# Segment attention on one core: loops over chunks of 512 rows beside one straight program for segments under 768 owners

## The chip, the cores and the metric

The kernel runs on one core of one Trainium2 chip. The metric is the device time of one execution in microseconds (us). The kernel before takes 1196.74 us, the median of three runs (1195.85 to 1197.27).

## The reference

Each of 16384 tokens has 256 features and one of 8 segment numbers, which are not sorted. Each segment has 3072 padded slots, and `pos` says which slot a token takes. Two tokens can claim one slot, and then the later one owns it.

```python
q, k, v = feat @ Wq, feat @ Wk, feat @ Wv          # 32, 32 and 256 columns
starts = jnp.searchsorted(bids, jnp.arange(8))
pos = jnp.arange(N) - starts[bids]
qp, kp, vp = pad(q), pad(k), pad(v)                # .at[bids, pos].set
scores = jnp.where(mask[:, None, :], qp @ kp.T, -1e9)
r = (softmax(scores) @ vp)[bids, pos]              # per segment
t = r @ Wt
tn = (t - t.mean(0)) / jnp.sqrt(t.var(0) + 1e-5) * gamma + beta
return feat + relu(tn)
```

## The kernel before

All arithmetic is in 32-bit floats, and a matmul of this type stands in the trace as two rows, called passes below. There are three stages.

**Preparation** (L66 to L323). The index arithmetic runs on VectorE: starts by a binary search, positions, owners of slots, the row that each token reads (`ridx`, L323), and per segment the number of owners `n_bc` and of chunks `nch` (L274). A table `t_rows` in DRAM is filled with zeros by DMAs of 2432 KB each on GpSimd's queue (L117); TR (L63) sets how many. GpSimd's index constants (L122) stand behind the fills in its program, and VectorE waits for them (L123). Wv is multiplied by Wt, so that the attention gives t directly.

**Attention, by segment** (L325 to L481). The number of chunks of 512 rows is loaded into a register of every engine (L338), and two sets of loops run over it. The first loop (L346), once for each chunk, finds the tokens that own the chunk's rows: comparisons with a counter (L351, L352), matmuls `pc` (L371), and short VectorE work (L373 to L381). Four indirect DMAs fetch their features (L385). They are transposed on TensorE (`px`, L397) and multiplied into q and k (`pqk`, L401) and into v times Wt (`pv`, L409). The second pair of loops runs over chunks of queries (L425) and, inside it, over chunks of keys (L430). In each pass of the inner loop, four tiles of 128 queries go through the chain that L434 to L463 write: scores `s` with queries on partitions, their maximum `nm` on VectorE (L438), the exponential `pr` on ScalarE with its sum (L445), four transposes `pT` (L451) and a copy `prT` (L453), so that the keys come onto partitions, four matmuls `po` (L456), and a rescaled sum `acc` (L463). Behind the loop over keys the sum is divided (L467, L470) and stored to `t_rows` (L479).

**Normalisation** (L483 to L541). 128 indirect DMAs on GpSimd fetch every token's row (L510), while matmuls with ones add them up (`ps_m`, L498). Then come the subtraction of the mean (L523), squares (L525) and their sums (`ps_v`, L498), and the output with residual (L538 to L541).

The order inside a loop body is that of a list scheduler, and a loop's body is a scheduling unit of its own: nothing crosses from one pass or one segment to the next.

Of the kernel before, what the change touches and what calls it, by code (L numbers as in the profile page):

```python
# [9 lines left out]
F32 = mybir.dt.float32  # L10
I32 = mybir.dt.int32
# [13 lines left out]
CAP = (LMAX // CH + 1) * CH  # rows kept for a segment: its tokens and at least one zero row  # L25
# [3 lines left out]
def segment_attention_bn_kernel(  # L29
# [23 lines left out]
    J = N // P  # tokens of a partition: token = p * J + j  # L53
# [25 lines left out]
    with ExitStack() as att:  # L79
        keep = att.enter_context(tc.tile_pool(name="keep", bufs=1))  # L80
        # Inclusive counts of a segment's owners along each partition's tokens, then the count in
        # the partitions before, then the partition's first token.
# [10 lines left out]
        with ExitStack() as prep:  # L93
# [7 lines left out]
            PS = LMAX // J  # LMAX tokens are PS partitions  # L101
# [10 lines left out]
            # Rows of the table that no segment fills have values too.  # L112
# [22 lines left out]
            # tri[k, m] = k < m; shift[k, m] = (k == m + PS)  # L135
# [20 lines left out]
            # ---- starts: a binary search by segment, over partitions' first tokens, then over  # L156
            # one partition's tokens ----
# [118 lines left out]
            # A segment's first row: those before it have n + 1 rows each.  # L276
# [49 lines left out]
        seg = att.enter_context(tc.tile_pool(name="seg", bufs=1))  # L326
        work = att.enter_context(tc.tile_pool(name="work", bufs=2))
        qT = seg.tile([DQ, CAP], F32, name="qT")
        kT = seg.tile([DQ + 1, CAP], F32, name="kT")  # and what the mask adds to a key's scores
        vx = seg.tile([P, CAP // P, D], F32, name="vx")  # L330
        qw = seg.tile([DQ + 1, CH], F32, name="qw")  # a chunk of queries, and ones for the mask
        nc.vector.memset(qw[DQ : DQ + 1, :], 1.0)
        acc = seg.tile([P, CT, D], F32, name="acc")
        den = seg.tile([P, CT], F32, name="den")
        nmax = seg.tile([P, CT], F32, name="nmax")  # minus the maximum so far

        for b in range(NB):
            n_chunks = nc.values_load(  # L338
                nch[0:1, b : b + 1],
                min_val=1,  # L340
                max_val=CAP // CH,
                skip_runtime_bounds_check_because="a segment has at most LMAX owners of slots",
            )

            with tc.tile_pool(name=f"psA{b}", bufs=2, space=PSUM) as psA:
                with tc.For_i(0, n_chunks) as c:  # L346
                    ir = iota_r[:, ds(c * CH, CH)]
                    # Which partition holds the token of a row, then which of its tokens.
                    oh = work.tile([P, CH], F32, tag="oh", name=f"oh{b}")
                    ge = work.tile([P, CH], F32, tag="ge", name=f"ge{b}")  # L350
# [4 lines left out]
                    # Rows of no token: an index out of bounds, for which zeros stay.  # L355
                    pad = work.tile([P, CT], F32, tag="pad", name=f"pad{b}")
                    nc.vector.tensor_scalar(
                        pad, rcol[:, ds(c * CT, CT)], n_bc[:, b : b + 1], float(N),
                        ALU.is_ge, ALU.mult,
                    )  # L360
                    nc.vector.tensor_scalar(
                        kT[DQ : DQ + 1, ds(c * CH, CH)],
                        iota_r[DQ : DQ + 1, ds(c * CH, CH)],
                        n_bc[DQ : DQ + 1, b : b + 1], NEG, ALU.is_ge, ALU.mult,
                    )
                    x = work.tile([P, CT, D], F32, tag="x", name=f"x{b}")
                    nc.gpsimd.memset(x, 0.0)  # L367
                    idx = work.tile([P, CT], I32, tag="idx", name=f"idx{b}")
                    for t in range(CT):
                        pc = psA.tile([P, J + 2], F32, tag="pc", name=f"pc{b}")  # L370
                        nc.tensor.matmul(pc, oh[:, ts(t, P)], lcx[:, b, :], start=True, stop=True)  # L371
                        lr = work.tile([P, 1], F32, tag="lr", name=f"lr{b}")
                        nc.vector.tensor_tensor(  # L373
                            lr, rcol[:, ds(c * CT + t, 1)], pc[:, J : J + 1], ALU.subtract
                        )
                        upto = work.tile([P, J], F32, tag="upto", name=f"upto{b}")
                        jc = work.tile([P, 1], F32, tag="jc", name=f"jc{b}")
                        nc.vector.tensor_scalar(
                            upto, pc[:, 0:J], lr, None, ALU.is_le, ALU.add, accum_out=jc
                        )  # L380
                        nc.vector.scalar_tensor_tensor(  # L381
                            idx[:, t : t + 1], pc[:, J + 1 : J + 2], jc, pad[:, t : t + 1],
                            ALU.add, ALU.add,
                        )
                        nc.gpsimd.indirect_dma_start(  # L385
                            out=x[:, t, :],
                            out_offset=None,
                            in_=feat,
                            in_offset=bass.IndirectOffsetOnAxis(ap=idx[:, t : t + 1], axis=0),
                            bounds_check=N - 1,  # L390
                            oob_is_err=False,
                        )
                    xT = work.tile([P, DH, CH], F32, tag="xT", name=f"xT{b}")
                    for h in range(DH):
                        px = psA.tile([P, CH], F32, tag="px", name=f"px{b}")
                        for t in range(CT):
                            nc.tensor.transpose(px[:, ts(t, P)], x[:, t, ts(h, P)], ident)  # L397
                        nc.scalar.copy(xT[:, h, :], px)
                    pqk = psA.tile([2 * DQ, CH], F32, tag="pqk", name=f"pqk{b}")
                    for h in range(DH):  # L400
                        nc.tensor.matmul(  # L401
                            pqk, wqk[:, h, :], xT[:, h, :], start=(h == 0), stop=(h == DH - 1)
                        )
                    nc.vector.tensor_copy(qT[:, ds(c * CH, CH)], pqk[0:DQ, :])
                    nc.vector.tensor_copy(kT[0:DQ, ds(c * CH, CH)], pqk[DQ : 2 * DQ, :])
                    for t in range(CT):
                        pv = psA.tile([P, D], F32, tag="pv", name=f"pv{b}")
                        for h in range(DH):
                            nc.tensor.matmul(  # L409
                                pv, xT[:, h, ts(t, P)], wvt[:, h, :],  # L410
                                start=(h == 0), stop=(h == DH - 1),
                            )
                        nc.scalar.copy(
                            vx[:, ds(c * CT + t, 1), :].rearrange("p x d -> p (x d)"), pv
# [162 lines left out]
```

## Time and profile before

| what | us |
| --- | --- |
| median of three runs | 1196.74 |
| span of the profiled execution, first to last instruction | 1179.1 |
| median less span | 17.6 |
| preparation, to the last index (L323) | 0 to 76.5 |
| attention, to the last division (L470) | 77.5 to 824.6 |
| gathering of rows and mean | 829.1 to 1000.7 |
| variance | 1000.7 to 1063.5 |
| output | 1063.5 to 1179.1 |
| TensorE busy over the span | 699.6 |
| VectorE, ScalarE, GpSimd busy | 454.2, 165.3, 212.9 |

The execution that was profiled has only its span as a time of its own; the runs' times are taken without a profile and contain 17.6 us beside such a span. Rows of groups give busy time, the mean duration of one instruction in ns, and the idle time of the engine ahead of it with what ended it. Rows of the timeline give start, duration, engine, line, and in brackets the idle time ahead of it. PE is TensorE's matmuls, PEld its weight loads, DVE VectorE, ACT ScalarE, POOL GpSimd, SP SyncE. PEclk is the granted clock of TensorE, 1.00 being full.

### The profile page before, as it was taken

Reading aid. Unit: us, or ns where it says so; the run is one execution under the profiler, and the core shown is the slowest. Engines: PE = TensorE matmul, PEld = TensorE weight load, DVE = VectorE, ACT = ScalarE, POOL = GpSimd, SP = SyncE. Lnnn points to the kernel's source line nnn. Section 1 sums busy time; section 2 is a strip of 40 time slices with the busy share of each in tenths; the row PEclk is TensorE's granted clock in tenths of the full one; section 3 lists DMA queues with packets and bytes.
Section 4 is the critical chain, followed back from the end, with each engine's and each line's share of the span. In section 5 each row is a group of like instructions: output and inputs, shape, how many; then the busy total and the mean of one; then the engine's idle time right before and its main releaser. Section 6 shows DMA issues by size and latency. Waiting matters only on the chain. (4 is left out here: it accounts for less than half of the span.)

```text
span 1179.1 us, 9985 instructions
## 1 busy us (share of the span) xinstructions
PE 699.6 (59%) x1835; PEld 365.8 (31%) x1835; DVE 454.2 (39%) x1028; ACT 165.3 (14%) x375; POOL 212.9 (18%) x220
## 2 busy tenths in 40 slices
PE   2028465867568684686657765747577776990000
PEld 1015233444334452254434434424111111340000
DVE  4863233334324332333332334223000000918998
ACT  0002010212112220121102211202000000540000
POOL 4010103000110001100030000110677775000000
PEclk9998676787767786687866877668555565895555
DMA  9910100000100001000000000010333332003896
GB/s 348 333 66 1 37 19 19 1 18 0 35 8 1 18 0 37 7 0 19 18 25 1 1 18 18 15 35 1 103 99 101 103 99 84 1 0 142 303 329 258
DMA packets 25441, 80.12 MB, mean 68 GB/s; under 512 B 4674, under 2 KB 11819, under 8 KB 21301
## 3 DMA queue, kind: packets, MB, share of 16 engines
q0 software_dynamic: 12816, 38.85, 10.4%
q1 hardware_dynamic: 8901, 23.19, 6.0%
q10 hardware_dynamic: 3680, 17.63, 3.7%
q14 instruction: 33, 0.27, 0.1%
q8 instruction: 11, 0.18, 0.1%
HBM read 40.82 MB, written 40.50 MB: 69 GB/s over the span
## 5 line engine op out<-in xcount | busy, mean ns | idle before, releaser
L456 PE MATMUL po<-vx,prT 128*128 x640 | 188.4, 452 | 14.6 <-ACT prT L453 14.6
L456 PEld LDWEIGHTS po<-vx,prT 128*128 128x128 f32 x640 | 138.4, 225 | 85.6 <-issue 33.1
L434 PE MATMUL s<-kT,qw 33*128 x160 | 120.9, 869 | 68.3 <-DVE den L428 53.5
L498 PE MATMUL ps_m<-tt,ones 128*128 128x512 f32 x128 | 125.4, 1083 | 52.4 <-DMA tt<-t_rows,ridx 52.2
L510 POOL DMA_INDIRECT tt<-t_rows,ridx x128 | 127.6, 997 | 65.9 <-issue 65.9
L463 DVE SCALAR_TENSOR_TENSOR acc<-acc,fade,po 128x256 f32<-128x256 f32 x80 | 38.4, 480 | 132.7 <-PE po L456 132.7
L371 PE MATMUL pc<-lcx,oh 128*128 128x130 f32 x96 | 29.9, 465 | 98.7 <-DVE oh L352 92.0
L438 DVE TENSOR_REDUCE nm<-s 128x1 f32<-128x512 f32 x80 | 55.3, 691 | 82.6 <-PE s L434 82.5
L498 PEld LDWEIGHTS ps_m<-tt,ones 128*128 128x128 f32 x128 | 30.9, 299 | 145.7 <-issue 103.5
L367 POOL MEMSET x<- 128x1024 f32 x12 | 11.4, 951 | 351.0 <-PEq L338 223.9
L492 DVE COPY mean<-ps_m 128x256 f32<-128x256 f32 x1 | 0.4, 424 | 174.8 <-PE ps_m L498 174.8
L451 PE MATMUL pT<-ident,pr 128*128 128x128 f32 x320 | 59.6, 332 | 13.1 <-ACT pr L445 13.1
L434 PEld LDWEIGHTS s<-kT,qw 33*128 33x128 f32 x160 | 33.3, 243 | 100.6 <-DVE den L428 58.3
L451 PEld LDWEIGHTS pT<-ident,pr 128*128 128x128 f32 x320 | 49.0, 176 | 45.3 <-ACT pr L445 38.5
L429 POOL MEMSET acc<- 128x1024 f32 x12 | 11.4, 951 | 281.1 <-POOLq L425 193.0
L498 PE MATMUL ps_v<-sq,ones 128*128 128x512 f32 x128 | 58.2, 619 | 5.6 <-ACT sq L525 5.6
L385 POOL DMA_INDIRECT x<-in_r_feat,idx x48 | 48.1, 1001 | 72.1 <-DVE idx L381 61.4
L397 PE MATMUL px<-ident,x 128*128 128x128 f32 x96 | 32.5, 444 | 46.1 <-DMA x<-in_r_feat,idx 46.0
L525 ACT ACTIVATE sq<-tt 128x2048 f32<-128x2048 f32 x16 | 30.6, 1910 | 204.8 <-DVE tt L523 184.1
L441 ACT ACTIVATE fade<-nmax,nm 128x1 f32<-128x1 f32 x80 | 23.5, 294 | 240.2 <-DVE nm L439 240.1
L371 PEld LDWEIGHTS pc<-lcx,oh 128*128 128x128 f32 x96 | 22.8, 312 | 106.9 <-DVE oh L352 86.4
L445 ACT ACTIVATE pr<-s,nm 128x512 f32<-128x512 f32 x80 | 53.4, 668 | 0.0
(166 smaller groups left out, 671.2 us busy)
## 6 DMA issues: line engine op xcount, KB each, us to landing
t_rows<-zero POOLq DMA_DIRECT2D x7, 2432.0 KB, 37.5
f<-in_r_feat SPq DMA_DIRECT2D x16, 1024.0 KB, 7.4
out<-y ACTq DMA_DIRECT2D x16, 1024.0 KB, 7.6
t_rows<-tq SPq DMA_DIRECT2D x12, 512.0 KB, 3.0
tt<-t_rows,ridx POOLq DMA_INDIRECT x128, 2.8
x<-in_r_feat,idx POOLq DMA_INDIRECT x48, 2.8
wv_sb<-in_L_rec_Wv ACTq DMA_DIRECT2D x1, 256.0 KB, 13.5
wt_sb<-in_L_rec_Wt ACTq DMA_DIRECT2D x1, 256.0 KB, 18.8
```

The source lines that it names most:

```text
L371: nc.tensor.matmul(pc, oh[:, ts(t, P)], lcx[:, b, :], start=True, stop=True)
L385: nc.gpsimd.indirect_dma_start(out=x[:, t, :], out_offset=None, in_=feat, in_offset=bass.IndirectOffsetOnAxis(ap=idx[:, t : t + 1], axis=0 ...
L397: nc.tensor.transpose(px[:, ts(t, P)], x[:, t, ts(h, P)], ident)
L434: nc.tensor.matmul(s, qw[:, ts(t, P)], kT[:, ds(kc * CH, CH)], start=True, stop=True)
L438: nc.vector.tensor_reduce(nm, s, AX.X, ALU.max, negate=True)
L445: nc.scalar.activation(pr, s, AF.Exp, bias=nm, accum_out=rsum)
L451: nc.tensor.transpose(pT[:, ts(u, P)], pr[:, ts(u, P)], ident)
L456: nc.tensor.matmul(po, prT[:, ts(u, P)], vx[:, ds(kc * CT + u, 1), :].rearrange("p x d -> p (x d)"), start=(u == 0), stop=(u == CT - 1),)
L463: nc.vector.scalar_tensor_tensor(acc[:, t, :], acc[:, t, :], fade, po, ALU.mult, ALU.add)
L498: nc.tensor.matmul(ps, ones, x[:, 2 * h : 2 * h + 2, :], start=(g == 0 and h == 0), stop=(g == J // GT - 1 and h == GT // 2 - 1),)
L510: nc.gpsimd.indirect_dma_start(out=tt[g][:, i, :], out_offset=None, in_=t_rows, in_offset=bass.IndirectOffsetOnAxis(ap=ridx[:, j : j + 1], ...
L525: nc.scalar.activation(sq, tt[g], AF.Square)
```

## The change

The attention stage is written a second time, for segments of fewer than FW = 768 owners, as one program without loops. The largest number of owners is reduced from `n_bc` and loaded into a register of every engine; if it is under 768, the new program runs. It gathers the reciprocals of all denominators in `rdens`, and behind the last segment counts those that are not between 1e-30 and 1e30 into `bad`. `bad` is 1 ahead of the test, so that it also stands for the case of a longer segment. Then `bad` is loaded on every engine, and the code of before runs only if it is over 0. The table grows by 256 rows before rounding, which makes eight fills of it in place of seven.

In the new program each segment has 768 rows (FT = 6 tiles of 128) whatever its owners, and two chunks of 384 queries (QC). Scores are computed with keys on partitions, so `pr` needs no transposes. The exponential takes no maximum, and what masks the keys beyond the owners is its bias per partition. Queries beyond the owners are set to zero. A column of ones in `v` gives the denominator as column 257 of `po`. All six key tiles add up in one PSUM tile, so `acc`, `fade` and `den` go. Segments are interleaved: `project(b + 1)` and `load_rows(b + 2)` stand ahead of `attend(b)`.

```diff
-    TR = -(-(N + NB + CH) // (P * FB)) * P * FB
+    TR = -(-(N + NB + FW) // (P * FB)) * P * FB
...
+        bad = keep.tile([P, 1], I32, name="bad")
+        nc.vector.memset(bad, 1)
+        nc.vector.tensor_reduce(longest, n_bc[0:1, :], AX.X, ALU.max)
+        nc.vector.tensor_copy(longest_i, longest)
+        n_max = nc.values_load(longest_i[0:1, 0:1], ...)
+        with tc.If(n_max < FW):
+                ps_a = short.enter_context(tc.tile_pool(name="ps_a", bufs=1, space=PSUM))
+                ps_s = short.enter_context(tc.tile_pool(name="ps_s", bufs=3, space=PSUM))
+                ps_o = short.enter_context(tc.tile_pool(name="ps_o", bufs=2, space=PSUM))
+                xs = [fs.tile([P, FT, D], F32, name=f"xs{i}") for i in range(2)]
+                vs = [fs.tile([P, FT, D + 1], F32, name=f"vs{i}") for i in range(2)]
...
+                def load_rows(b):
+                    nc.vector.tensor_scalar(ge, ir, lcx[:, b, J : J + 1], None, ALU.is_ge)
+                    nc.vector.scalar_tensor_tensor(oh, ir, cend[:, b : b + 1], ge, ALU.is_lt, ALU.mult)
...
+                    for h in range(FT // 3):
+                        pc = ps_a.tile([P, 3, J + 2], F32, tag="pc", name=f"pc_{b}")
+                        for t in range(3):
+                            nc.tensor.matmul(pc[:, t, :], oh[:, ts(3 * h + t, P)], lcx[:, b, :], ...)
...
+                    for t in range(FT):
+                        nc.gpsimd.indirect_dma_start(out=x[:, t, :], in_=feat, ...)
+                def project(b):
+                    for c in range(FT // 2):
+                        for h in range(DH):
+                            px = ps_a.tile([P, 2 * P], F32, tag="px", name=f"px_{b}", bufs=2)
+                            for t in range(2):
+                                nc.tensor.transpose(px[:, ts(t, P)], x[:, 2 * c + t, ts(h, P)], ident)
+                            if h == 0:
+                                nc.scalar.copy(xT[:, h, ts(c, 2 * P)], px)
+                            else:
+                                nc.vector.tensor_copy(xT[:, h, ts(c, 2 * P)], px)
+                    for c in range(FW // QC):
+                        pqk = ps_a.tile([2 * DQ, QC], F32, tag="px", name=f"pqk_{b}", bufs=2)
...
+                        nc.vector.scalar_tensor_tensor(q[:, own], iota_r[0:DQ, own], n_bc[0:DQ, b : b + 1], pqk[0:DQ, :], ALU.is_lt, ALU.mult)
+                        nc.scalar.copy(k[:, own], pqk[DQ : 2 * DQ, :])
+                    for c in range(FT // 2):
+                        pv = ps_a.tile([P, 2, D], F32, tag="px", name=f"pv_{b}", bufs=2)
...
+                        nc.scalar.copy(v[:, 2 * c : 2 * c + 2, 0:D], pv)
+                def attend(b):
+                    for c in range(FW // QC):
+                        for t in range(FT):
+                            s = ps_s.tile([P, QC], F32, tag="s", name=f"s_{b}")
+                            nc.tensor.matmul(s, k[:, ts(t, P)], q[:, ts(c, QC)], start=True, stop=True)
+                            nc.scalar.activation(pr[:, t, :], s, AF.Exp, bias=mask[:, t : t + 1])
+                        for u in range(QC // P):
+                            po = ps_o.tile([P, D + 1], F32, tag="po", name=f"po_{b}")
+                            for t in range(FT):
+                                nc.tensor.matmul(po, pr[:, t, ts(u, P)], v[:, t, :], ...)
+                            nc.vector.reciprocal(rden, po[:, D : D + 1])
+                            nc.vector.tensor_scalar(tq[:, u, :], po[:, 0:D], rden, None, ALU.mult)
...
+                        nc.sync.dma_start(t_rows[ds(first_row, QC), :].rearrange("(t p) d -> p t d", p=P), tq)
+                load_rows(0)
+                project(0)
+                load_rows(1)
+                for b in range(NB):
+                    if b + 1 < NB:
+                        project(b + 1)
+                    if b + 2 < NB:
+                        load_rows(b + 2)
+                    attend(b)
...
+        again = nc.values_load(bad[0:1, 0:1], ...)
+        with tc.If(again > 0):
...
```

What the change does to the order is shown at three places. The first is TensorE in the inner loop over keys: before, the body of the first segment, from its first scores on (`s` scores, `pT` transposes of exponentials, `po` the products with v; ISA rows set addresses from registers).

```order
L434 MATMUL s_500<-kT,qw 128x512
L434 ISA
L434 MATMUL s_525<-kT,qw 128x512
L451 MATMUL pT_512<-ident,pr_508 128x128 x4
L434 MATMUL s_550<-kT,qw 128x512
L456 ISA
L456 MATMUL po_519<-vx,prT_517 128x256
```

After, the same place is a stretch of the straight program, around `attend(2)` (`pv` belongs to the fourth segment, `pc` to the fifth, `px` to the gathered features of the fifth).

```order
L448 MATMUL pv_1024<-wvt,xT_975 128x256 x4
L383 MATMUL pc_1056<-lcx,oh_1031 128x130 x3
L471 MATMUL s_1107<-q_788,k_789 128x384
L477 MATMUL po_1111<-vs_373,pr_1091 128x257 x6
L477 MATMUL po_1120<-vs_373,pr_1091 128x257 x6
L477 MATMUL po_1129<-vs_373,pr_1091 128x257 x6
L471 MATMUL s_1140<-q_788,k_789 128x384
L477 MATMUL po_1177<-vs_373,pr_1139 128x257 x6
L423 MATMUL px_1188<-ident,xs_371 128x128 x2
```

The transposes between scores and products are gone, six products follow each other into one tile, and matmuls of three segments stand behind one another without a branch. (Rows that only repeat are left out: five more `s` ahead of each group of `po`.)

The second place is GpSimd's queue in the preparation: before, the fills of the table and the index constants behind them.

```order
L117 DMA t_rows<-zero 2432x1x256 x7
L122 IOTA tok_i 128x128
L122 IOTA irow_i 128x128
L122 IOTA pcol_i 128x1
L122 IOTA ecol_i 128x8
```

After, the same rows:

```order
L121 DMA t_rows<-zero 2432x1x256 x8
L126 IOTA tok_i 128x128
L126 IOTA irow_i 128x128
L126 IOTA pcol_i 128x1
L126 IOTA ecol_i 128x8
```

One more fill stands ahead of the constants that VectorE waits for. The third place is VectorE at the end of the attention: before, the last division is followed by the ends of the two loops and the mean of the next stage.

```order
L467 RECIPROCAL rden_2378<-den 128x4
L470 TENSOR_SCALAR tq_2380<-acc,rden_2378 128x256 x4
L425 REGISTER_ALU
L425 COMPARE_AND_BRANCH
L425 UNCONDITIONAL_BRANCH
L492 COPY mean<-ps_m 128x256
```

After, the count of bad denominators and the branch over the old code follow the last division.

```order
L484 TENSOR_SCALAR tq_2047<-po_2066,rdens 128x256
L507 TENSOR_SCALAR below_lim<-rdens 128x48
L510 SCALAR_TENSOR_TENSOR good,odd<-rdens,below_lim 128x48
L513 TENSOR_SCALAR odd<-odd 128x1
L516 CAST bad<-ps_bad 128x1
L344 UNCONDITIONAL_BRANCH x2
L519 TENSOR_LOAD bad
L525 COMPARE_AND_BRANCH
```

Every engine has the load of `bad` and the branch, GpSimd too, whose gathers of the next stage stand right behind them. The instructions of the normalisation are the same, in the same order, on each engine.

More of the change, by code (lines that the diff above doesn't have):

```diff
@@ L323, in segment_attention_bn_kernel @@
             nc.vector.tensor_copy(ridx, row)
[L326 to L350, printed above, removed]
+        bad = keep.tile([P, 1], I32, name="bad")
@@ L366, in segment_attention_bn_kernel @@
[L366 to L372, printed above, removed]
+                        gone, rcol[:, 0:FT], n_bc[:, b : b + 1], None, ALU.is_ge
+                    )
@@ L392, in segment_attention_bn_kernel @@
                         )
[L393 to L407, printed above, removed]
+                    parts[b] = mask
@@ L473, in segment_attention_bn_kernel @@
-                    first_row = nc.s_assert_within(
-                        base_b + qc * CH,
-                        min_val=0,
-                        max_val=TR - CH,
-                        skip_runtime_bounds_check_because="a chunk begins at one of its segment's rows",
-                    )
-                    nc.sync.dma_start(
-                        t_rows[ds(first_row, CH), :].rearrange("(t p) d -> p t d", p=P), tq
-                    )
+                        nc.vector.tensor_copy(qT[:, ds(c * CH, CH)], pqk[0:DQ, :])
@@ L484, in segment_attention_bn_kernel @@
+            lng.close()
     GT = 8
```

322 lines of the change are left out of this document (253 added, 69 removed).

## The prediction

> **What bounds the kernel now.** I read the slices of the page first, then busy times by stage, then the groups by line and the timeline of one loop body.
>
> ```profile
> PE   2028465867568684686657765747577776990000
> PEclk9998676787767786687866877668555565895555
> ```
>
> ```profile
> core 0: us, PE busy (x) PEld busy (x) DVE busy (x) ACT busy (x) POOL busy (x), PEclk, DMA share, GB/s
> 77.50:824.60 747.10, 506.19 (x1552) 303.77 (x1552) 254.45 (x801) 130.15 (x352) 69.94 (x71) 0.74 0.05 14
> 829.10:1000.70 171.60, 125.37 (x128) 30.93 (x128) 1.14 (x3) 0.00 (x0) 127.61 (x128) 0.55 0.33 98
> ...
> 850.00:890.00 40.00, 31.79 (x32) 7.52 (x30) 0.00 (x0) 0.00 (x0) 30.82 (x31) 0.50 0.34 102
> 1011.00:1063.00 52.00, 52.00 (x122) 22.83 (x120) 25.05 (x12) 26.11 (x14) 0.00 (x0) 1.00 0.00 0
> ```
>
> The attention takes 747.1 of 1179.1 us. TensorE is the busiest engine there, but busy for only 506.2 us, at a mean clock of 0.74: the stage loses time to gaps and to a slow clock, and it is the only stage that the change rewrites. How many passes it makes is in the groups.
>
> ```profile
> L456 PE MATMUL po<-vx,prT 128*128 x640 | 188.4, 452 | 14.6 <-ACT prT L453 14.6
> L438 DVE TENSOR_REDUCE nm<-s 128x1 f32<-128x512 f32 x80 | 55.3, 691 | 82.6 <-PE s L434 82.5
> L445 ACT ACTIVATE pr<-s,nm 128x512 f32<-128x512 f32 x80 | 53.4, 668 | 0.0
> L367 POOL MEMSET x<- 128x1024 f32 x12 | 11.4, 951 | 351.0 <-PEq L338 223.9 <-PE pc L371 49.7 <-POOLq L346 46.6
> ```
>
> 12 clearings of `x` are 12 chunks, and 80 maxima are 20 inner passes of four tiles: with eight segments, four have one chunk and four have two (4 + 4x4 = 20). So four segments have 512 to 1023 owners, which does not say whether all are under 768. Counting owners by the reference's rule on its own inputs gives 431 to 726, so the new program runs; its largest score is 36.4, and sums of exponentials stay between 3e4 and 7e15, inside the limits of the count.
>
> **The steady state of the new program.** Its 36.1 us for a segment come from passes at full clock.
>
> ```profile
> 231.17 3.72 PE L456 MATMUL po<-vx,prT 128*128 x16
> 234.72 0.60 PE L451 MATMUL pT<-ident,pr 128*128 128x128 f32 x4
> 277.56 1.04 PE L451 MATMUL pT<-ident,pr 128*128 128x128 f32 x8
> 278.53 1.12 PE L434 MATMUL s<-kT,qw 33*128 x2
> 1057.91 0.19 PEld L498 LDWEIGHTS ps_v<-sq,ones 128*128 128x128 f32 x1 [0.24 <-issue]
> 1058.34 0.19 PEld L498 LDWEIGHTS ps_v<-sq,ones 128*128 128x128 f32 x1 [0.24 <-issue]
> ```
>
> 16 passes of 256 columns take 234.72 - 231.17 = 3.55 us, 0.222 each; passes of 512 columns start 1058.34 - 1057.91 = 0.43 us apart; eight transposes take 1.04, 0.13 each; a weight load takes 0.19. Per segment, two passes to a matmul: `s` 12 matmuls of 384 columns, 24 passes of 0.33 (0.43 x 384/512, and a little) = 7.9; `po` 36 matmuls of 257, 72 x 0.223 = 16.1; `pv` 12 matmuls, 24 x 0.222 = 5.3; `pqk` 4 matmuls, 8 x 0.33 = 2.6; `pc` 6 matmuls of 130 columns, 12 passes which the weight load bounds, at 0.22 (estimate, 0.19 and an issue gap) = 2.6; `px` 12 transposes, 1.6. Sum 36.1.
>
> The other engines stay below that. The stage before had ScalarE busy for 130 us and VectorE for 254 (row 77.50:824.60). The exponentials shrink from 80 x 512 to 96 x 384 columns, and VectorE loses the maxima, half of the `prT` copies and `acc`; so both lie under the 8 x 36.1 = 289 us of TensorE. GpSimd needs 6 indirect DMAs for each segment, 6 x 1.3 = 7.8 us (rows at 81.47 and 82.86 below).
>
> The waits inside a segment: two PSUM buffers serve `px`, `pqk` and `pv`, and each must be copied out before its next use. Going through a segment with these durations in the order of the program, TensorE waits only among the transposes, where VectorE's index work stands between two copies: about 1 us a segment. From `pv` on, three buffers of `s`, and exponentials that take less than the 0.66 us of a score (0.668 for 512 columns), keep it fed. So seven segments with their successor's projection take 7 x (36.1 + 1), the last one 7.9 + 16.1: 283.7 us.
>
> **The ends.** Three terms are added around it: the start, the fill, and the exit.
>
> ```profile
> 1.54 8.23 POOL L117 DMA_DIRECT2D t_rows<-zero  x6
> 21.68 1.32 POOL L117 DMA_DIRECT2D t_rows<-zero  x1 [11.91 <-issue]
> ...
> 23.30 3.46 DVE L123 CAST tok<-tok_i 128x128 f32<-128x128 int32 x1 [10.67 <-POOL tok_i L122]
> ...
> 76.28 0.23 DVE L323 CAST ridx<-row 128x128 int32<-128x128 f32 x1
> 77.53 0.49 DVE L351 TENSOR_SCALAR ge<-iota_r,lcx 128x512 f32 x1 [1.03 <-issue]
> ```
>
> ```profile
> DMA to landing us min/median/max: 19.8/37.5/51.1
> ```
>
> The first six fills are issued at once, the seventh only at 21.68 us, just when the first has landed (1.54 + 19.8 = 21.3); the constants follow it, and VectorE waits 10.67 us for them. So the eighth fill will wait for the second to land. The fourth was issued near 1.54 + 3 x 8.23/6 = 5.7 and, with the median, landed near 43.2, so fills land (43.2 - 21.3)/3 = 7.3 us apart, and the chain of index work, which has no slack behind L123, starts **7.3 us later** (bounds 0, and the 11.9 of the seventh). This is a cost of the change that no other work covers. The preparation then ends at 76.3 + 7.3, and with the 1.2 us from L323 to the first `ge` (the load of a register and a branch stand there too now) the attention begins at 84.8.
>
> ```profile
> 78.96 1.21 PE L371 MATMUL pc<-lcx,oh 128*128 128x130 f32 x4 [9.99 <-DVE oh L352]
> 81.47 1.09 POOL L385 DMA_INDIRECT x<-in_r_feat,idx  x1 [22.77 <-DVE idx L381]
> 82.86 1.03 POOL L385 DMA_INDIRECT x<-in_r_feat,idx  x1 [0.30 <-DVE idx L381]
> 84.49 0.66 PE L397 MATMUL px<-ident,x 128*128 128x128 f32 x2 [2.48 <-DMA x<-in_r_feat,idx]
> 89.46 3.63 PE L401 MATMUL pqk<-xT,wqk 128*64 128x512 f32 x4 [0.51 <-ACT xT L398]
> ```
>
> The first segment has nothing to hide behind. From the first `ge` to the first gather it was 81.47 - 77.53 = 3.9 us; with 768 columns and the comparisons of later segments in between, 7.3. Six gathers take 7.8, and 1.1 because the second half of the indices stands behind a copy of transposed features on VectorE; landing and transposing 84.49 - 81.47 + 0.5 = 3.5. `pqk` and `pv` come after an idle time, where a pass of 512 columns took 3.63/4 = 0.9, half speed: 7.9 us at full clock, up to 16 at half, 13 taken. The fill is 32.7 us (22 to 40).
>
> ```profile
> 819.62 2.00 PE L456 MATMUL po<-vx,prT 128*128 x8 [0.73 <-ACT prT L453]
> ...
> 829.07 1.00 POOL L510 DMA_INDIRECT tt<-t_rows,ridx  x1 [27.16 <-issue]
> ```
>
> ```profile
> 774.90 1.14 DVE L470 TENSOR_SCALAR tq<-acc,rden 128x256 f32<-128x256 f32 x4
> 780.55 0.95 POOL L367 MEMSET x<- 128x1024 f32 x1 [27.49 <-PEq L338]
> ```
>
> The exit before, from the end of the last `po` to the first gather of the next stage, is 829.07 - 821.62 = 7.5 us. Now it has one division (0.5), the count (three VectorE instructions, a matmul, a copy: 2, estimate), and the load of `bad` with a branch on every engine. The nearest row is a segment's end, 780.55 - 776.04 = 4.5 us of loop ends, load and branch. The branch goes past all of the old code, which no row shows: 0 to 4.5 more, of which I take 2. Sum 9. The Trainium skill, page "Runtime: NRT & Kernel Launch", section "Instruction fetch mechanics", says that a taken branch to code not yet fetched stalls; no run here shows that alone, and it gives no price.
>
> The sum: 84.8 + 32.7 + 283.7 + 9 = 410.2 for the first gather, where it was 829.1. Behind it nothing changes: 1179.1 - 829.1 = 350.0. The span is 760, 419 less, and with the 17.6 us between span and median, **778 us**.
>
> **The rivals.** *The clock drops in every projection.* In 850:890 TensorE was busy for 79% of the time, with gaps of about 0.6 us, and still had half clock throughout, so short gaps suffice to keep it slow. A projection (`px`, `pc`, `pqk`, `pv`: 12.1 us) has such gaps at its head; if it ran at half clock each time, 7 x 12.1 = 85 us are added: 863. Against it speaks that transposes at 277.56 were followed by full-speed scores at 278.53, so a full clock outlives a microsecond of transposes. The Trainium skill, page "TensorE: Matmul & The Clock Gate", section "Part 4: PE-mode transpose", says that transposes do not count as TensorE being busy, which would make this rival the case; its table "Why this matters for your kernels" allows gaps up to about 3 us, which the half clock of 850:890 contradicts.
>
> *Each segment is bound by copies out of PSUM:* if the waits come to 9 us in place of 1, 7 x 8 = 56 more: 834. For it: two buffers, and three waits that cross engines for each.
>
> *Half clock throughout:* 283.7 becomes 567, total 1061. Against it: the dense stretch 1011:1063 ran at 1.00.
>
> *The old code still runs, and the kernel is slower.* If one segment had 768 owners or more, the new program is skipped, and before's time with the eighth fill and two branches results, 1197 + 7 + 5 = 1209. If a single denominator lay outside the limits, both run: 778 + 747 = 1525. The owners and scores counted above speak against both.
>
> **How the numbers follow.** The forecast has a chance of 0.78, copies 0.09, clock in projections 0.07, half clock throughout 0.03, old code 0.03. The forecast alone is uncertain by the bounds above: down by 7.3 (fill DMA), 11 (pipeline fill), 4 (exit) and 7 (waits), not all at once: 750; up to 805 with the upper bounds and waits of 3 us a segment. The range reaches on to the second rival: 748 to 840. All but the old code are faster by far more than 0.2%, about what a measurement can tell from no change: 0.965; slower 0.03; 0.005 is left for no difference, which no case gives.
>
> **What would show it.** Right: one group `po` of 576 passes (8 x 72) near 223 ns apart, PEclk at 1.00 from about 120 us to 400, the first `tok` copy near 30.6 us, gathers of `t_rows` starting near 410, and no rows of the loops. Wrong: PEclk falling at each `px`, waits of TensorE on `xT` or `vs` copies of over 3 us a segment, or rows of the old code.

## The result and the profile after

The changed kernel takes **780.44 us** (four runs, 779.17 to 782.01); the kernel before took 1197.01 beside it on the same chip: ratio 0.6518 [0.6503, 0.6534]. 778 was forecast. The profiled execution took 781.66 us with a span of 779.8: 1.9 us lie outside the span, not the 17.6 of the prediction. So the total fits better than its terms: the span is 20 us longer than the 760 of the sum.

The page's slices show TensorE full, and its clock near full, from the sixth of the 40 slices to the twentieth, where before both were ragged.

```profile
PE   0201299999999999999973777775335999000000
PEclk9999999899999989999895555556556899555555
```

Busy times by stage: the filling of the pipeline, the attention from the second segment's transposes to the last output pass, the gathering with the mean, and a part of it.

```profile
core 0: us, PE busy (x) PEld busy (x) DVE busy (x) ACT busy (x) POOL busy (x), PEclk, DMA share, GB/s
84.10:113.10 29.00, 19.04 (x69) 13.33 (x70) 15.81 (x61) 3.23 (x7) 14.94 (x16) 1.00 0.12 35
113.10:403.70 290.60, 290.42 (x1149) 209.97 (x1147) 69.72 (x257) 82.68 (x153) 35.88 (x36) 0.94 0.10 34
413.10:599.00 185.90, 120.37 (x128) 31.88 (x128) 0.03 (x1) 0.00 (x0) 127.66 (x128) 0.54 0.31 90
542.00:586.00 44.00, 16.22 (x17) 4.60 (x16) 0.00 (x0) 0.00 (x0) 28.92 (x29) 0.50 0.30 90
```

In the attention TensorE is busy for 290.42 of 290.60 us: nothing is waited for any more. But the mean clock is 0.94, not 1.00. (The 1.00 of the first row is no measurement: the clock's records in this trace begin at 106.4 us. Six passes of `pc` take 1.64 us at 86.75 and 0.83 at 125.38, so the filling ran at half clock up to there.) And from the first gather to the copy of `mean` there are 185.8 us, where the same code took 170.3 before. The timeline, in order of time, with start, duration, and in brackets the idle time before:

```profile
21.83 1.32 POOL L121 DMA_DIRECT2D t_rows<-zero  x1 [12.05 <-issue]
28.19 1.31 POOL L121 DMA_DIRECT2D t_rows<-zero  x1 [5.03 <-issue]
...
29.80 3.46 DVE L127 CAST tok<-tok_i 128x128 f32<-128x128 int32 x1 [17.28 <-POOL tok_i L126]
...
103.81 4.06 PE L436 MATMUL pqk<-xT,wqk 128*64 128x384 f32 x8
107.80 5.45 PE L448 MATMUL pv<-wvt,xT 128*128 128x256 f32 x24
...
128.91 8.10 PE L477 MATMUL po<-vs,pr 128*128 128x257 f32 x36
...
141.42 11.00 PE L477 MATMUL po<-vs,pr 128*128 128x257 f32 x36
152.26 0.60 PE L423 MATMUL px<-ident,xs 128*128 128x128 f32 x4
...
167.82 9.76 PE L477 MATMUL po<-vs,pr 128*128 128x257 f32 x36
...
181.60 9.70 PE L477 MATMUL po<-vs,pr 128*128 128x257 f32 x36
191.14 0.60 PE L423 MATMUL px<-ident,xs 128*128 128x128 f32 x4
...
403.72 0.17 DVE L483 RECIPROCAL rdens<-po 128x1 f32<-128x1 f32 x1 [1.92 <-PE po L477]
...
413.14 1.00 POOL L712 DMA_INDIRECT tt<-t_rows,ridx  x1 [90.70 <-issue]
```

The eighth fill is issued 6.4 us after the seventh, and `tok` is 6.5 us later than before (23.30). One segment takes 191.14 - 152.26 = 38.9 us. 36 passes of `po` take 8.10 us, or, as at 141.42, 11.00 with nothing waited for: there the clock fell to 0.5, by its records from 140.5 to 147.4 us. Then the stage that was not changed, first as it began and then as it went on:

```profile
435.59 2.04 PE L700 MATMUL ps_m<-tt,ones 128*128 128x512 f32 x2 [0.56 <-DMA tt<-t_rows,ridx]
438.19 2.04 PE L700 MATMUL ps_m<-tt,ones 128*128 128x512 f32 x2 [0.56 <-DMA tt<-t_rows,ridx]
...
564.27 1.01 PE L700 MATMUL ps_m<-tt,ones 128*128 128x512 f32 x1 [1.79 <-issue]
567.08 1.01 PE L700 MATMUL ps_m<-tt,ones 128*128 128x512 f32 x1 [1.80 <-issue]
...
578.54 0.99 POOL L712 DMA_INDIRECT tt<-t_rows,ridx  x1 [0.30 <-issue]
...
598.97 0.42 DVE L694 COPY mean<-ps_m 128x256 f32<-128x256 f32 x1 [193.40 <-PE ps_m L700]
```

At first two passes follow each pair of gathers, every 2.6 us. From 542 to 590 us a pass mostly starts only every 2.80 us, with no semaphore to wait for; TensorE falls behind, and `mean` follows the last gather by 20.4 us. In the profile of before that gap was 5.0:

```profile
994.44 0.99 POOL L510 DMA_INDIRECT tt<-t_rows,ridx  x1 [0.30 <-issue]
...
999.41 0.42 DVE L492 COPY mean<-ps_m 128x256 f32<-128x256 f32 x1 [174.83 <-PE ps_m L498]
```

### The profile page after: what moved, and what is told of

Its sections match the earlier page's. It is cut to its first block, busy times and chain, and to the rows that moved or that the text cites. A ratio compares the mean times of both kernels' runs of the same rounds, so it can differ in the third digit from the quotient of the medians.

```text
span 779.8 us, 4797 instructions
## 1 busy us (share of the span) xinstructions
PE 498.3 (64%) x1501; PEld 286.5 (37%) x1501; DVE 285.7 (37%) x555; ACT 120.9 (16%) x183; POOL 195.0 (25%) x201
## 5 line engine op out<-in xcount | busy, mean ns | idle before, releaser
L477 PE MATMUL po<-vs,pr 128*128 128x257 f32 x576 | 145.9, 417 | 0.0
L477 PEld LDWEIGHTS po<-vs,pr 128*128 128x128 f32 x576 | 119.5, 210 | 30.4 <-issue 5.4
L404 POOL DMA_INDIRECT xs<-in_r_feat,idx x48 | 48.5, 1010 | 187.5 <-PE pqk L436 122.0
L472 ACT ACTIVATE pr<-s,mask 128x384 f32<-128x384 f32 x96 | 55.7, 580 | 99.3 <-PE s L471 95.4
L471 PE MATMUL s<-q,k 32*128 32x384 f32 x192 | 70.6, 506 | 0.0
L448 PE MATMUL pv<-wvt,xT 128*128 128x256 f32 x192 | 43.6, 383 | 0.0
L448 PEld LDWEIGHTS pv<-wvt,xT 128*128 128x128 f32 x192 | 35.8, 190 | 9.3 <-ACT k L443 4.8
L740 DVE TENSOR_TENSOR y<-tt,scale 128x2048 f32<-128x2048 f32 x16 | 36.4, 2282 | 1.1 <-DMA out<-y 1.1
L742 DVE SCALAR_TENSOR_TENSOR y<-y,f 128x2048 f32<-128x2048 f32 x16 | 36.4, 2282 | 0.0
L741 DVE TENSOR_TENSOR y<-y,beta_bc 128x2048 f32<-128x2048 f32 x16 | 36.4, 2282 | 0.0
L383 PE MATMUL pc<-lcx,oh 128*128 128x130 f32 x96 | 17.6, 316 | 13.9 <-POOL vs L356 11.3
```

Source lines behind the costliest of these rows:

```text
L404: nc.gpsimd.indirect_dma_start(out=x[:, t, :], out_offset=None, in_=feat, in_offset=bass.IndirectOffsetOnAxis(ap=idx[:, t : t + 1], axis=0 ...
L448: nc.tensor.matmul(pv[:, t, :], xT[:, h, ts(2 * c + t, P)], wvt[:, h, :], start=(h == 0), stop=(h == DH - 1),)
L471: nc.tensor.matmul(s, k[:, ts(t, P)], q[:, ts(c, QC)], start=True, stop=True)
L472: nc.scalar.activation(pr[:, t, :], s, AF.Exp, bias=mask[:, t : t + 1])
L477: nc.tensor.matmul(po, pr[:, t, ts(u, P)], v[:, t, :], start=(t == 0), stop=(t == FT - 1),)
L740: nc.vector.tensor_tensor(y, tt[g], over_tokens(stat["scale"]), ALU.mult)
```

## The experiments

Runs of one group were made on one chip, with runs of the kernel before between them; the three groups ran on different chips. "After" below is the changed kernel. Across chips ratios to before are compared: in the first group with 0.6518 of the result, in the second and third with 0.6494 [0.6470, 0.6519], measured in the third. Differences in us between profiles are of one execution each.

### Where 17 us come and go

The kernel before, unchanged (first group):

> The kernel before, unchanged, to see where the 17.6 us between its span (1179.1) and its median come from. In the kernel after, each of four runs took only 1.9 us more than its span, and its profile shows passes of `ps_m` 2.80 us apart from 542 to 590 us, where before's profile has two passes in 2.6 us all the way. Theory A, the 17.6 us are mostly such a stretch, which the profiled execution of before happened not to have: a new span is 1194 to 1196 with a time 2 us longer, and the copy of `mean` has waited some 190 us instead of 174.8. Rival B, a fixed cost outside the span that only the long program with its loops has: the span is 1179 again, the time 1197.

1199.20 us over ten runs (1195.4 to 1202.6); the profiled one took 1199.61 with a span of 1197.8. Its timeline in the gathering stage:

```profile
976.63 1.01 PE L498 MATMUL ps_m<-tt,ones 128*128 128x512 f32 x1 [1.80 <-issue]
979.42 1.01 PE L498 MATMUL ps_m<-tt,ones 128*128 128x512 f32 x1 [1.78 <-DMA tt<-t_rows,ridx]
```

And its group of the copy of `mean`, with the idle time ahead of it:

```profile
L492 DVE COPY mean<-ps_m 128x256 f32<-128x256 f32 x1 | 0.4, 425 | 193.2 <-PE ps_m L498 193.2
```

Theory A holds: the same passes 2.80 us apart, 193.2 us of waiting in place of 174.8, and 1.8 us outside the span. And after, unchanged (third group):

> The kernel after, unchanged, as the yardstick for the three others on the same chip. If the slow stretch of `ps_m` is a matter of the chip (one chip so far showed it in all runs of before, 1198, another in none, 1182), this kernel and before carry it both or neither: 780 beside a before of 1198, or 762 to 765 beside 1182. Rival, the stretch comes with the dense attention of the kernel after: 780 here whatever before takes.

765.12 us (762.9 to 772.1), beside 1181.05 for before. Its gathering ends with pairs of passes 2.6 us apart, as in the first profile of before; behind the timeline stands the group of the copy:

```profile
562.80 2.05 PE L700 MATMUL ps_m<-tt,ones 128*128 128x512 f32 x2 [0.48 <-DMA tt<-t_rows,ridx]
```

```profile
L694 DVE COPY mean<-ps_m 128x256 f32<-128x256 f32 x1 | 0.4, 424 | 178.1 <-PE ps_m L700 178.1
```

So the stretch goes with the chip, not with the kernel: on the first group's chip all 17 runs of before took 1194.5 to 1203.8, on the two others all 20 took 1179.9 to 1186.1. Both kernels carry it or neither; the ratio is the same, 0.65, and the time of after is 780 or 765. Each chip was measured in one group only, so that something else that differed between the groups isn't ruled out, and what makes the stretch stays open.

### The fills of the table

> The kernel after with a table of 17024 rows, 7 fills as before. Theory, the eighth fill holds back the constants and with them all that follows: the first `tok` copy is at 23.3 us in place of 29.8, and the time is 6.5 us less, 774. Rival, the later start is taken up somewhere behind it (the first gathers wait for the fills to end in any case): less than 2 us, 779 to 780.

```diff
-    TR = -(-(N + NB + FW) // (P * FB)) * P * FB
+    TR = 7 * P * FB
```

779.22 us (773.9 to 781.5), ratio 0.6486 [0.6461, 0.6512]: 4 us under after by ratio, with intervals that overlap. The profile shows the start as expected and its loss on the way:

```profile
23.41 3.46 DVE L127 CAST tok<-tok_i 128x128 f32<-128x128 int32 x1 [10.80 <-POOL tok_i L126]
411.14 1.00 POOL L712 DMA_INDIRECT tt<-t_rows,ridx  x1 [94.00 <-issue]
```

`tok` is 6.4 us earlier, the first gather only 2.0: in this execution the clock's records show 12 falls in the attention in place of 8, 47.8 us at half clock in place of 37.5, which is 5 us lost. The term is right in the trace, and too small for the runs to settle against such falls.

> The kernel after with the fills issued behind the constants. Theory, the fills hold back VectorE by blocking GpSimd and nothing else needs that time: the search then starts when `ps_first` is there, at 17.2 us in place of 33.8, so 16 us less, 764. Rival, the fills then run into the transfers behind them, or VectorE waits for the weights that share the DMA engines with them: a gain under 8 us, 773 or more.

```diff
-            for k in range(TR // (P * FB)):
-                nc.gpsimd.dma_start(t_fill[k], zero.unsqueeze(1).to_broadcast([P, FB, D]))
...
             iota_f(rcol, [[P, CAP // P]], 0, 1, [P, CAP // P], "rcol_i")
+            for k in range(TR // (P * FB)):
+                nc.gpsimd.dma_start(t_fill[k], zero.unsqueeze(1).to_broadcast([P, FB, D]))
```

772.87 us (770.0 to 774.3), ratio 0.6444 [0.6425, 0.6463]: 9 us less, near the rival. `ridx` came 19.6 us earlier, but then stood a wait that was hidden before:

```profile
63.13 0.23 DVE L327 CAST ridx<-row 128x128 int32<-128x128 f32 x1
74.40 0.62 DVE L365 TENSOR_SCALAR ge<-iota_r,lcx 128x768 f32<-128x768 f32 x1 [11.04 <-DMA t_rows<-zero]
```

If the new stage's first buffers lie where the fills still read their zeros, keeping that tile takes the wait away (third group):

> The fills behind the constants, and the tile of zeros that they read moved to the pool that stays, since with the constants first the first `ge` waited 11.0 us for the last fill (its buffer lay in the memory of the fills' source). Theory, that wait was only this reuse: `ge` follows `ridx` at 64.4, the first gathers of `in_r_feat` start near 72, and the time is another 8 to 10 us below the kernel with the constants first alone, 18 below the unchanged one. Rival, the gathers stand behind the fills in GpSimd's DMA queue: they land only when the last fill has, near 74, and 2 to 8 us more is all.

```diff
-            zero = pp.tile([P, D], F32, name="zero")
+            zero = keep.tile([P, D], F32, name="zero")
```

744.57 us (744.1 to 752.0), ratio 0.6316 [0.6293, 0.6339], **20.5 us below after** on the same chip, where the theory had 18: the fastest version here. `ge` follows `ridx` with 1.3 us between, and the first gather of features (72.15) starts in time:

```profile
64.62 0.79 DVE L365 TENSOR_SCALAR ge<-iota_r,lcx 128x768 f32<-128x768 f32 x1 [1.29 <-issue]
```

### The branches

> The kernel after without the second branch and without the loops behind it: segments that fail the test or the count would stay uncomputed; these inputs don't need them. Theory, load, branch and jump are the exit of 9.5 us: the first gather of `t_rows` then waits for the landing of the last `tq`, issued at 404.4 and there about 2.5 us later, so it starts at 407 to 408 in place of 413.1: 5 to 6 us less, 775. Rival, the exit is the wait for that landing and the semaphores of the stage, and the branch costs under 1 us: 780. A second rival, that the long program's code also costs time elsewhere (its loading at the start, or beside the span): more than 8 us less.

774.07 us (772.0 to 775.4), ratio 0.6452 [0.6434, 0.6470]: 6 us below after by medians, 8 by ratio. The end of the attention in its timeline, the copy of the count and the first gather:

```profile
405.10 0.16 DVE L516 CAST bad<-ps_bad 128x1 int32<-128x1 f32 x1 [0.47 <-PE ps_bad L515]
...
408.16 1.00 POOL L545 DMA_INDIRECT tt<-t_rows,ridx  x1 [86.02 <-issue]
```

From the last output pass to the first gather are 4.8 us, of which the landing of the last `tq` is 2.5; after has 9.5. Load, branch and jump cost 4.7 that show; `ridx` comes at 82.4 (82.8 in after) and the time beside the span is 1.8 us as in after, so the long program costs nothing at the start or there.

> The kernel after with 512 in the test of the longest segment in place of 768, so that the straight program is skipped and the loops do the work; this prices the rival of the prediction that was to end on the slower side. By the prediction it is before's time and 12 us, 1209: 7 for the eighth fill, 5 for branches. Rival, skipped code costs nothing to jump over: 1204.

1200.67 us in one run, beside 1181.74 (nine runs, 1179.9 to 1185.3): 19 more, not 12. Against the first profile of before, the fill is 6.1 of it; `ge` follows `ridx` after 6.0 us (82.36 to 88.41) where before it was 1.25, which is 4.8. These two are near the 7 and 5 that were said. The other 8 to 9 lie behind them: 4 in the attention, 1 at its end, 3 ahead of the subtraction of the mean, where VectorE waits for no semaphore. VectorE at the skip:

```profile
82.36 0.23 DVE L327 CAST ridx<-row 128x128 int32<-128x128 f32 x1
87.53 0.48 DVE L533 MEMSET qw<- 1x512 f32 x1 [4.94 <-issue]
```

This is what the Trainium skill, page "Runtime: NRT & Kernel Launch", section "Instruction fetch mechanics", says of a taken branch to code not yet fetched, a stall; that this idle time is such a fetch is argued, not shown. Here there are 3.9 us of it over the 1.03 of before, with a second load and test in it.

### What made the attention dense

> The kernel after with each segment written as loading, projection, attention, with no work of the next written between. Theory, the order of the code is only a hint: the scheduler takes loads and projections as early as the two buffers allow, TensorE's stream keeps them between attentions, and only the cover of two scores among the transposes goes: 1 to 2 us a segment, 8 to 15 us more, about 792. Rival, the written order is what hides the projection: the 29 us from the first `ge` to the last `pv`, of which 12 are passes, come back in each segment: 7 x 17 = 119 more, 900.

```diff
-                load_rows(0)
...
                 for b in range(NB):
...
+                    load_rows(b)
+                    project(b)
                     attend(b)
```

795.40 us (793.7 to 796.8), ratio 0.6729 [0.6711, 0.6747]: 28 us more, far from the rival, twice the theory. Busy times over the whole attention, of after in the third group and of this kernel:

```profile
95.00:405.00 310.00, 303.25 (x1205) 219.59 (x1204) 77.54 (x292) 85.91 (x160) 45.57 (x46) 0.94 0.11 36
```

```profile
95.00:432.00 337.00, 320.20 (x1202) 229.48 (x1202) 76.89 (x288) 86.15 (x160) 45.41 (x46) 0.89 0.10 31
```

TensorE idles for 16.8 us in place of 6.8. The other 17 are the clock: 320.2 x 0.11 = 35 us lost to it in place of 303.3 x 0.06 = 18. So with ten more microseconds of gaps more was lost in clock than in gaps. This is one profile of each; the attention of after lost 24 in the profile with seven fills, so some 11 to 17 of it go with the new order. That the gaps cause the falls is argued.

> The kernel after as one straight program, but with queries on partitions as before: each tile of 128 queries has two scores of 384 keys, two maxima, exponentials with that maximum, six transposes and their copies; the owners past the end are masked by a 33rd row of keys. The check of the sums and the division are kept. Theory, the gain came from the straight program (only the needed lengths, no loop ends, scores of one tile beside the output passes of another), and the layout adds little: 36 transposes of 0.13 a segment = 4.7 us, and waits, 8 x 5 to 8 x 12 us: 820 to 880. Rival, the layout without maximum and transposes is what made TensorE dense: with the chain of maximum, exponential, transpose and copy back in each of 48 tiles, gaps and half clock return as before: over 1000.

```diff
+    nc.tensor.matmul(s[e], q[:, ts(w, P)], k[:, ts(e, QC)], start=True, stop=True)
+    nc.vector.tensor_reduce(nm[:, e : e + 1], s[e], AX.X, ALU.max, negate=True)
...
+    nc.scalar.activation(pr[:, ts(e, QC)], s[e], AF.Exp, bias=nm[:, 0:1])
...
+    nc.tensor.transpose(pT[:, ts(t, P)], pr[:, ts(3 * e + t, P)], ident)
...
```

961.40 us (959.9 to 961.8), ratio 0.8130 [0.8109, 0.8151]: 193 us more, between the two. One tile of 128 queries in its timeline:

```profile
407.90 0.91 PE L480 MATMUL s<-k,q 33*128 33x384 f32 x2
...
408.85 0.56 DVE L483 TENSOR_REDUCE nm<-s 128x1 f32<-128x384 f32 x1 [0.15 <-PE s L480]
...
410.37 1.05 ACT L489 ACTIVATE pr<-s,nm 128x384 f32<-128x384 f32 x2 [7.58 <-DVE nm L486]
...
411.00 1.02 PE L494 MATMUL pT<-ident,pr 128*128 128x128 f32 x6 [2.19 <-ACT pr L489]
...
412.13 0.56 DVE L496 COPY prT<-pT 128x384 f32<-128x384 f32 x1 [0.82 <-PE pT L494]
...
412.79 4.56 PE L501 MATMUL po<-vs,prT 128*128 128x257 f32 x12
```

The chain from a tile's second score over maximum, exponential, transposes and copy to its output passes holds TensorE up by 2.2 us here, and `po` runs at half clock (4.56 where 12 passes take 2.7). So the theory fell. The first gather of `t_rows`, in this kernel and in after (third group):

```profile
608.82 1.00 POOL L736 DMA_INDIRECT tt<-t_rows,ridx  x1 [141.20 <-issue]
```

```profile
410.15 1.00 POOL L712 DMA_INDIRECT tt<-t_rows,ridx  x1 [90.69 <-issue]
```

The straight program brings it from 829.1 to 608.8 (with 6.5 us of the fill against it), the layout from there to 410.2. **Each is about half of the gain.** "Straight program" stands here for all that this kernel has of the change: no loops, the interleaving, and one maximum and one sum for all 768 keys in place of the rescaling. The division holds for this path; the layout inside the loops was not run. And it holds for the order that the scheduler made, in which a tile's second score stands behind the output of the tile before; another order could shorten that chain.

### What hides the exponentials, and the clock

> The kernel after with each exponential computed twice into the same place (48 times 2 more a row of keys tile, 96 more of 580 ns, 55.7 us of ScalarE in all). Theory, ScalarE's idle time lies in other places than where it is needed: six scores take TensorE 4.13 us and their exponentials 3.5, so doubled they end about 7.0 + 0.6 after the first score, 3 us behind the last one, in each of 16 halves: 48 us more. Rival, ScalarE with 99 us of idle time ahead of the exponentials alone hides it: under 5 us more.

774.86 us (773.6 to 776.1): 9.7 more than after on the same chip, between both. TensorE in one half:

```profile
180.75 3.10 PE L471 MATMUL s<-q,k 32*128 32x384 f32 x8
183.77 1.14 PE L478 MATMUL po<-vs,pr 128*128 128x257 f32 x4
184.84 1.55 PE L471 MATMUL s<-q,k 32*128 32x384 f32 x4
186.32 7.22 PE L478 MATMUL po<-vs,pr 128*128 128x257 f32 x32
```

The scheduler puts the last two scores behind the first passes of `po`, and a pass of `po` needs only its own tile of `pr`. So the exponentials have the scores and the first output passes to hide behind, and doubled they make a half 0.6 us longer (12.8 from the first score to the last product, where after's halves without a fall of the clock take 12.2), not 3.

> The kernel after with the transposes of the features made as ordinary matmuls against the identity. In the kernel after the granted clock falls to 0.5 for 3.4 or 6.8 us eight times within the attention, 37.5 us in all, always while passes of `po` run. Theory A, the falls belong to the dense passes themselves: they stay (5 to 12 of them), and the 96 transposes as two passes each cost 96 x 0.13 = 12 us, less what the index work covers: 0 to 12 us more. Theory B, transposes do not count as work for the clock (the Trainium skill, page 'TensorE: Matmul & The Clock Gate', section 'Part 4: PE-mode transpose') and the falls are their late effect: no falls are left, and of 14 to 19 us gained 12 are paid: 0 to 15 us less.

```diff
-                                nc.tensor.transpose(
-                                    px[:, ts(t, P)], x[:, 2 * c + t, ts(h, P)], ident
-                                )
+                                nc.tensor.matmul(
+                                    px[:, ts(t, P)], x[:, 2 * c + t, ts(h, P)], ident,
+                                    start=True, stop=True,
+                                )
```

779.56 us (775.1 to 782.7): 14.4 more than after. The records show 12 falls of the clock in the attention (9 in after's profile of this group), and over it:

```profile
95.00:418.00 323.00, 321.16 (x1298) 239.08 (x1297) 76.94 (x285) 86.25 (x160) 45.74 (x46) 0.92 0.10 33
```

Theory B falls: without a single transpose in the attention the clock falls no less often (12 falls stood also in the kernel with seven fills, which has the transposes). The time is a little over the 0 to 12 of theory A. That transposes don't count as work (the Trainium skill, page "TensorE: Matmul & The Clock Gate", section "Part 4: PE-mode transpose") is not their cause here. The kernel without lookahead, with more gaps, has 14; why they come in a TensorE that is busy all the time is not settled.

### The mean on VectorE

> The kernel after with the sums for the mean made by VectorE while the rows arrive, and 4 passes of TensorE at the end in place of 128 all along. Theory, the tail from the last gather (578.5) to the copy of `mean` (599.0) is the slow stretch of the passes of `ps_m`: now only landing (2.6), a last addition (2.3), half of one (1.2) and 4 passes at half clock (4.1) follow the gather's 1.0, so the copy is at 589.7 and the time 9 us less, 771. Rival A, the slow stretch belongs to that time and not to `ps_m`: the passes of `ps_v` then go at 2.8 us for a while, no gain or a loss. Rival B, VectorE's additions hold up GpSimd: the gathers come more than 1.30 us apart, and 0.1 us more for each is 13 us.

```diff
-        add_up(ps_m, tt[g], g)
...
+            nc.vector.tensor_add(total, total, tt[g])
...
+        nc.tensor.matmul(
+            ps_m, ones, total[:, 2 * h : 2 * h + 2, :], start=(h == 0), stop=(h == 1)
+        )
```

780.24 us (779.3 to 780.7), ratio 0.6595 [0.6580, 0.6609]: 12 us more than after. This chip had no slow stretch to win back; the theory's gain could not show. Rival B did:

```profile
427.91 2.29 DVE L722 TENSOR_TENSOR total<-tt,tt 128x2048 f32<-128x2048 f32 x1 [31.57 <-DMA tt<-t_rows,ridx]
428.20 2.87 POOL L713 DMA_INDIRECT tt<-t_rows,ridx  x1 [0.30 <-issue]
```

A gather issued during an addition is done 0.87 us after its end (430.20 to 431.07) in place of 1.00 after its own start; 15 such additions stretch the gathers from 165.4 to 183.2 us. Unplanned, the sums took one of the buffers of `f`, so that its loads at the start went away, and the eighth fill was issued at 21.42 in place of 28.19: the first gather of `t_rows` came at 404.76 (410.15 in after's profile of the third group), so the additions cost more than the 12.

## Why the prediction was right

- **The start**: 7.3 us for the eighth fill; 6.5 in the profile. The attention begins at 84.06; 84.8 was said.
- **The fill of the pipeline**: 32.7; it is 29.0. `pqk` and `pv` took 4.06 + 5.45 = 9.5 us in place of 13: the first four passes of `pqk` still stand 0.65 us apart, the rest runs at full clock, although TensorE had waited before.
- **The steady state**: 283.7; it is 290.6, with two errors against each other. A segment without falls of the clock takes 38.9 less 3.3 (its two halves of `po` took 9.76 and 9.70 in place of 8.10), 35.6, where 37.1 was said: the 1 us of waits is not there, and `pc` takes 1.8 in place of 2.6 (0.15 a pass, so the weight load of 0.19 does not bound it), but `s` 4.13 a half in place of 3.95. 7 x 35.6 and 24.5 for the last are 273.7. The other 16.9 are the clock, 0.94 x 290.6 = 273. That a dense TensorE keeps 1.00, taken from a stretch of 52 us, is what failed here.
- **The exit**: 9; it is 9.5. The removal of the branch shows 4.7 of it, and 4.8 stay.
- **The rest**: 350.0 in the span and 17.6 beside it; it is 366.7 and 1.9. **This step failed twice, with opposite signs.** The 17.6 were taken for a fixed time beside the span. They were a stretch of slow passes of `ps_m` on the chip of the timed runs, which the profiled execution of before had not had. That the chip of the result had the stretch too, now inside the span, made the sum fit, and that is luck: on the other chips 765 stands against 778. What the prediction had right is the attention with its ends: 410.2 was said for the first gather, and it is 413.1.
- **The rivals**: the clock did not drop in projections (`pqk` 2.79 and `pv` 5.45 in later segments); its falls come elsewhere and cost a fifth of the 85 us. No copy out of PSUM is waited for: TensorE idles for 0.18 us in 290.6. The old code is skipped; had it run in place of the new, it would have cost 19 us, not 12: the fill (6.1) and the branches (4.8) had their price in the sum, and 8 to 9 us in the stages behind had none. Where those come from is open.
- **Where the gain lies** the prediction did not divide. On the path that was run, the straight program and the layout bring about half each.

## What to carry to other kernels

A profile's span and the median of other runs may differ by an event of a chip, not by a fixed overhead: before the gap is added as a constant, look whether an execution's own time exceeds its span by as much. When a dense engine bounds a stage, count its passes and allow some per cent for the clock (its mean was 0.94 and 0.92 here); a gap of TensorE can cost more than its own length, since more may be lost in clock (11 to 17 us beside 10 of gaps). What is issued first on a queue that can block (here fills ahead of constants) delays everything behind it, and when it is moved, the memory that it reads must not be reused by the stage that is to start early.

## What the runs showed of the hardware

- On the chip of the result and on that of the first group, about 120 us into a stage at half clock with TensorE busy for 78%, its passes came one per 2.80 us for about 50 us, in the first profile of after and in those of all four kernels of the first group, with a recorded clock of 0.50 as ahead of it; on the chips of the other groups it never came. The Trainium skill, page "TensorE: Matmul & The Clock Gate", section "Seeing it yourself", warns that the clock's records are unreliable and that the gate was seen stuck at a quarter of the clock for 50 us and more. The length agrees; the 2.80 us do not, since a quarter of the clock would make 4 x 0.43 = 1.7 us of a pass (estimate). No run here shows more of the cause.
- The granted clock falls to 0.5 for 3.4 or 6.8 us at a time in a TensorE without gaps, 8 to 12 times in some 290 us (after, and with 7 fills).
- An addition of two operands on VectorE (2.29 us) holds up an indirect DMA of GpSimd to its end and 0.87 us beyond. The Trainium skill, page "SBUF — State Buffer", section "Who interferes with whom", says that a VectorE instruction with two SBUF inputs contends with a GpSimd instruction that reads SBUF; the trace agrees, with the indices of the gather as what GpSimd would read (that is argued, not shown). The same section tells of a probe in which `tensor_tensor` did not stall a DMA; here it did.
- At the jump over skipped code VectorE idled for 4.94 us, with two loads and tests in it; ahead of the first `ge` of before, one load and test without such a jump cost 1.03.
